# Queries and keys of seven unpadded heads to an output, their rows sent to padded tiles; scores in six banks

## The chip, the cores and the metric

The kernel runs on one core of a Trainium2 chip. The metric is device time in microseconds (us), the median of three runs. Engines are named as in the profile: PE is TensorE (matrix products), PEld its weight loads, DVE is VectorE, ACT is ScalarE, POOL is GpSimd and SP is SyncE, which here issues most DMA transfers. SBUF has 128 partitions; the accumulators (PSUM) have eight banks of 128 x 512 f32 values.

## The reference

The input x is 4 sequences (B) of 512 tokens (T) with 288 features (C), all in f32, with one condition vector for each sequence. Four layers follow one another:

- layer 0: a conditioned block whose feed-forward part is a mixture of four experts, two of them used by each token;
- layer 1: a conditioned block with a dense feed-forward part;
- layer 2: a rotation of each token within a subspace of 64 dimensions, by a matrix exponential of the condition;
- layer 3: a conditioned block like layer 1, with weighted layer norms.

The change touches the attention, which is the same in layers 0, 1 and 3 (H = 16 heads of D = 18 features):

```
h   = layernorm(x) * (1 + scale) + shift            # scale, shift, gate from the condition
q, k, v = h @ Wq + bq, h @ Wk + bk, h @ Wv + bv      # each (4, 512, 288), cut into 16 heads of 18
a   = softmax(q @ k^T / sqrt(18))                    # (4, 16, 512, 512)
x   = x + gate * ((a @ v) @ Wp + bp)
```

## The kernel before

**Tiling.** Tokens come in tiles of P = 128 (NT = 4 to a sequence). Features stand transposed, in three chunks: two of 128 rows (MC = 2) and a remainder of RR = 32, which is kept four times, once on each strip of 32 partitions (`rows_of`, line 237). A product over all features is therefore a product with 32 rows and two with 128.

**Rounds.** The attention works in 16 rounds r, one for each pair of a sequence b and a group g of four heads (NG = 4, GH = 4). A head is padded from 18 to DP = 32 rows, so four heads fill 128 partitions and head i of the group stands on strip i. Round r computes, one round ahead, the queries and keys of round r + 1 (`queries_and_keys`, line 969): two outputs of 128 rows (s = 0 queries, s = 1 keys), each one product with the remainder and four with 128 rows over half of the tokens. ACT adds the bias and copies the output to a tile that has already the padded layout (line 996).

**Scores.** The maximum of a row is subtracted before the exponential, and by a trick: the keys have a row of ones at the padding row D, and `shift` (line 1053) turns the maxima over and subtracts them from the padding row of the queries. So the scores are computed twice: `row_max` (line 1002) has queries against keys, with DVE taking the maximum, and `weight` (line 1015) has keys against the shifted queries, with ACT taking the exponential. Each is one product of 32 rows with 512 columns in a bank of its own, of the tag "sc", which has four banks. The tag "de" has three, for all other products, and one bank ("av") holds the sums.

**Order.** A round has 8 gaps k. Every product that goes through `mm` is chained to the one before it, so PE's order is that of the code. Each gap begins with a quad: `quad` (line 1028) takes the two row maxima of gap k and two weights that lag by 9 gaps, in turn. A half quad n covers token tile n // 2 and heads n % 2 * 2 and n % 2 * 2 + 1:

```
for k in range(2):
    for what, r, n in halves:
        t, i = n // 2, n % 2 * 2 + k
...
quad([(row_max, r, k)] + lagging(8 * r + k - 9))
```

After the quad come the steps of the gap (layer norms, divisions and so on for DVE and POOL), then in gaps 1 and 5 the `sums` (line 1038: weights times values, four heads on four strips of columns), and then other products by a string such as "QQQ" or "XX", each letter one step of a job: Q is queries and keys, A the transposed activations of the next sequence, X the values or a projection. `shift` of a round stands at its end, behind gap 7. `others` (line 1174) writes these plans. Values (line 937) and projections (line 1139) take two token tiles at a time in two "de" banks, with their two remainder products beside each other on two strips.

**After the sums.** `collect` (line 1083) sends the rows of each head from the padded layout to an unpadded one, by transfers on POOL's queue; `invert` and `divide` normalise; `project` multiplies with Wp and adds to x through DVE and POOL.

**Weights.** `attention_weights` (line 253) loads them by SP. The host pads the columns of Wq and Wk to 32 a head, so their tile has 2 x 1024 columns. The weights of layers 1 and 3 are loaded during the feed-forward stage ahead of them, those of layer 0 at the start.

Of the kernel before, what the change touches and what calls it, by code (L numbers as in the profile page):

```python
# [23 lines left out]
HC = P // D  # L24
OR = 64
# [21 lines left out]
def kernel(ctx: ExitStack, tc: tile.TileContext, a: dict, out: bass.AP):  # L47
# [19 lines left out]
    banks = {"sc": 4, "de": 3}  # L67

    def bank(tag, name):
        return psum.tile([P, 512], F32, tag=tag, name=name, bufs=banks[tag])  # L70
# [104 lines left out]

    cT = cst.tile([CP, KC, B], F32, tag="cT", name="cT")
# [75 lines left out]

    def attention_weights(l):

        w = {}
        w["qk"] = wt.tile([P, MC, 2 * NG * P], F32, tag="wqk", name=f"wqk{l}")
        w["qkr"] = wt.tile([2 * RR, NG * P], F32, tag="wqkr", name=f"wqkr{l}")
# [3 lines left out]
        w["bqk"] = wt.tile([P, 2 * NG], F32, tag="bqk", name=f"bqk{l}")  # L261
# [7 lines left out]
        def qk():  # L269
            load(w["bqk"], a[f"bqk{l}"])  # L270
            full_chunks(w["qk"], a[f"wqk{l}"])
# [6 lines left out]
        def qk_rest():  # L278
            for s in range(2):
                remainder(w["qkr"], a[f"wqk{l}"][:, :, s * NG * P : (s + 1) * NG * P], [s])  # L280

        def projection(g):
# [4 lines left out]
        return w, [  # L287
            qk,
            qk_rest,
            lambda: full_chunks(w["v"], a[f"wv{l}"]),  # L290
            lambda: remainder(w["v"][:, MC], a[f"wv{l}"], range(P // RR)),
            whole_rows,
        ] + [lambda g=g: projection(g) for g in range(NG)]
# [622 lines left out]
    def attention(l, w, mod, eps, feed, ticks, hT=None, then=None, also=()):  # L916
# [11 lines left out]
        with ExitStack() as es:  # L928
            pool = es.enter_context(tc.tile_pool(name=name, bufs=2))
            hTs, xns, vs, qks, raws, outs, gbs = {}, {}, {}, {}, {}, {}, {}  # L930
            dens, ps = {}, {}
# [5 lines left out]
            def values(b, t0):  # L937

                yield
                if t0 == 0:  # L940
                    vs[b] = pool.tile([P, NT, H, D + 1], F32, tag="v", name=f"{name}v{b}")
                    nc.gpsimd.memset(vs[b][:, :, :, D : D + 1], 1.0)
                ps = [bank("de", f"{name}psv{b}_{t0 + n}") for n in range(2)]

                def product(n, c):
                    q = slice((t0 + n) * P, (t0 + n + 1) * P)
                    mm(
                        ps[n][:, 0:C],
                        lhsT=rows_of(hTs[b], c, n, q),
                        rhs=rows_of(w["v"], c, n, slice(0, C)),  # L950
                        start=(c == MC),
                        stop=(c == MC - 1),
                    )

                for n in range(2):
                    product(n, MC)
                for n in range(2):
                    for c in range(MC):
                        yield
                        product(n, c)  # L960
                    o = vs[b][:, t0 + n, :, 0:D]
                    i = ps[n][:, 0:C].rearrange("p (h d) -> p h d", d=D)
                    if "bv" in w:
                        bv = w["bv"].rearrange("p (h d) -> p h d", d=D)
                        nc.vector.tensor_add(o, i, bv)
                    else:
                        nc.vector.tensor_copy(o, i)

            def queries_and_keys(r):

                yield
                b, g = groups[r]
                ps = [bank("de", f"{name}psqk{r}_{s}") for s in range(2)]
                for s in range(2):
                    rows = slice(s * RR, (s + 1) * RR)
                    mm(
                        ps[s],
                        lhsT=w["qkr"][rows, g * P : (g + 1) * P],
                        rhs=hTs[b][rows, MC, :],
                        start=True,  # L980
                        stop=False,
                    )
                for s in range(2):
                    j = s * NG + g
                    for q in (slice(0, T // 2), slice(T // 2, T)):
                        for c in range(MC):
                            yield
                            mm(
                                ps[s][:, q],
                                lhsT=w["qk"][:, c, j * P : (j + 1) * P],  # L990
                                rhs=hTs[b][:, c, q],
                                start=False,
                                stop=(c == MC - 1 and q.stop == T),
                            )
                    t = pool.tile([P, T], F32, tag=f"qk{s}", name=f"{name}qk{r}_{s}", bufs=tags["qk0"])
                    nc.scalar.activation(t, ps[s], AF.Identity, bias=w["bqk"][:, j : j + 1])  # L996
                    qks[r, s] = t
# [4 lines left out]
            def row_max(r, t, i):  # L1002
# [5 lines left out]
                    lhsT=qks[r, 0][heads_rows(i), t * P : (t + 1) * P],  # L1008
                    rhs=qks[r, 1][heads_rows(i), :],
# [5 lines left out]
            def weight(r, t, i):  # L1015
# [3 lines left out]
                    lhsT=qks[r, 1][heads_rows(i), t * P : (t + 1) * P],  # L1019
                    rhs=qks[r, 0][heads_rows(i), :],  # L1020
# [32 lines left out]
            def shift(r):  # L1053
# [12 lines left out]
                q = qks[r, 0]  # L1066
# [72 lines left out]
            def project(b, t0):  # L1139

                yield
                o = outs[b, "o"]
                ps = [bank("de", f"{name}pp{b}_{t0}_{n}") for n in range(2)]

                def product(n, c):
                    t = t0 + n * NT // 2
                    if c < MC:
                        rows, q = slice(0, HC * D), c * T + t * P  # L1150
                    else:
                        rows, q = slice(n * OR, n * OR + (H - MC * HC) * D), MC * T + t0 * P
                    mm(
                        ps[n][:, 0:C],
                        lhsT=o[rows, q : q + P],
                        rhs=w["p"][rows, c, :],
                        start=(c == MC),
                        stop=(c == MC - 1),
                    )

                for n in range(2):
                    product(n, MC)
                for n in range(2):
                    for c in range(MC):
                        yield
                        product(n, c)
                    t = t0 + n * NT // 2
                    add_gated(ps[n][:, 0:C], gbs[b], b * NT + t, f"{name}r{b}_{t}")
# [5 lines left out]
            def others(r):  # L1174
# [7 lines left out]
                pieces = {0: "QQ", 2: "QQQ", 3: "QQQ", 4: "XQX", 6: "XX", 7: "X"}  # L1182
# [9 lines left out]
                if r + 1 < n:  # L1192
                    jobs["Q"] = queries_and_keys(r + 1)
# [7 lines left out]
                if g == 1 and b + 1 < B:  # L1201
                    jobs["A"] = activations(b + 1)
                    jobs["X"] = values(b + 1, 0)
                    pieces = {0: "QQA", 2: "QQQ", 3: "QQQ", 4: "QAA", 6: "XXX", 7: "XX"}
                if g == 2 and b + 1 < B:
                    jobs["X"] = values(b + 1, 2)


                if g == 2 and 0 < b <= B:
                    steps[1].append(lambda: divide(b - 1, 0))  # L1210
                    steps[2].append(lambda: divide(b - 1, 1))
                    steps[3].append(lambda: divide(b - 1, 2))
                if 0 <= r - 2 < n:
                    steps[4].append(lambda: invert(r - 2))
                if g == 3 and b > 0:
                    jobs["X"] = project(b - 1, 0)
                if g == 0 and b > 1:
                    jobs["X"] = project(b - 2, 1)
                if "X" not in jobs:
                    pieces = {0: "QQ", 2: "QQ", 3: "QQ", 4: "QQ", 6: "Q"}  # L1220
                if "Q" not in jobs:
                    pieces = {0: "X", 2: "X", 3: "X", 4: "X", 6: "X"}
# [18 lines left out]
            def places_of_first():  # L1241

                for f in range(NF):
                    q = f * feed.width % T
                    if q == 0:
                        n = f * feed.width // T
                        tag = f"qk{n % 2}" if n < 4 else "p"
                        t = pool.tile([P, T], F32, tag=tag, name=f"{name}f{f}", bufs=tags[tag])
                    yield t[:, q : q + feed.width]

            tags = {"qk0": 3, "qk1": 3, "p": 10}

            loads = feed.loads(l)
            first = [queries_and_keys(0)]
# [17 lines left out]
            jobs["X"], jobs["Y"] = values(0, 0), values(0, 2)  # L1272
            started(jobs)
            for t, pieces in enumerate(("QQQQ", "QQQQQ", "XXXXX", "YYYYY")):
# [6 lines left out]
            shift(0)  # L1281
            for r in range(1, n):
                jobs, pieces, steps = others(r)
# [3 lines left out]
                for k in range(gaps):  # L1287
                    quad([(row_max, r, k)] + lagging(8 * r + k - 9))
                    for step in steps[k]:
                        step()  # L1290
                    if k == 1 and r > 1:
                        sums(r - 2, 2)
                        sums(r - 2, 3)
                    if k == 5:
# [3 lines left out]
                    if k == gaps - 1:  # L1298
# [3 lines left out]
                        shift(r)  # L1302
# [4 lines left out]

            jobs, _, steps = others(n)
            jobs["A"] = feed.activations()
            started(jobs)  # L1310
            for k in range(NT + 1):
                quad(lagging(8 * n + 2 * k - 9) + lagging(8 * n + 2 * k - 8))
# [24 lines left out]
            for t in range(NT // 2):  # L1337
                drain(project(B - 1, t))
# [195 lines left out]
    class Dense(Feed):  # L1534
# [4 lines left out]
        def __init__(self, l, mod, eps, func, store):  # L1539
# [5 lines left out]
            self.hTs, self.gbs = {}, {}  # L1545
# [18 lines left out]
        def event(self, b, f):  # L1564

            if b + 1 < B and f == 2:
# [18 lines left out]
    class Experts(Feed):  # L1585
# [400 lines left out]
        def beside(self, r, jobs, pieces, spaced):  # L1986
# [18 lines left out]
            if r == 15:  # L2005
                pieces = {0: "X", 2: "XX", 3: "XX"}
# [402 lines left out]
    w, loads = attention_weights(0)  # L2409
    for load in loads:  # L2410
# [8 lines left out]
    w, loads = attention_weights(1)  # L2419
    mod, work = modulation(1)  # L2420
    aside.append(work)
    hT, also = feed.finish(1, mod, 1e-6, loads)
# [4 lines left out]
    w, loads = attention_weights(3)  # L2427
# [115 lines left out]
```

## Time and profile before

| what | value |
|---|---|
| runs | 1925.31, 1916.68, 1925.64 us; median 1925.31 |
| the profiled execution | 1924.44 us, of it a span of 1922.7 us on the core |
| granted PE clock | 0.988 of full speed |
| PE busy | 1871.0 us (97%) |
| DVE, ACT, POOL busy | 1068.9 us (56%), 737.4 us (38%), 528.4 us (27%) |
| layer 0's attention | about 25 to 412 us of the span |
| layer 1's attention | about 850 to 1204 us |
| layer 3's attention | about 1407 to 1757 us |

The page gives busy times by engine, and groups of instructions by line, engine and tile; the rows of the score products are called a0m, a0s (a1m, a3m and so on) after layer and kind, those of the outputs for queries and keys a0psqk, of the values a0psv, of the projections a0pp, of the sums av. All products have one line (79), that of the helper `mm`, so they are told apart by tile. In the timeline a line has its start, its length, engine, operation, and "out<-in" with partitions x columns. A matrix product in f32 leaves two records. Ends of PE's records are modelled, so intervals are read from start to start. In answers by windows a row has the stretch, its length, the busy time of PE, PEld, DVE, ACT and POOL (with the count of instructions), the granted clock, the share of the DMA engines and GB/s.

### The profile page before, as it was taken

To read this page: it belongs to the slowest core of one execution; us is meant where nothing else is said; L and a number is where in the kernel's file an instruction comes from. 1 tells how busy PE (TensorE), PEld (TensorE's weight loads), DVE (VectorE), ACT (ScalarE), POOL (GpSimd) and SP (SyncE) were. 2 spreads that over 40 slices of the span, in tenths; PEclk is the share of its full clock that TensorE was granted. 3 is DMA by queue.
4 is the path that set the end of the run, shared out by engine and by line. 5 is a ranking of instruction groups with operands and counts; after the bars stand their busy time and mean duration, and the time that the engine had idled before them with its cause. 6 is when DMAs were issued, how large, how long until landed. Compare 5 with 4: busy or idle time off the path is not lost. (4 is left out here: it accounts for less than half of the span.)

```text
span 1922.7 us, 28265 instructions
## 1 busy us (share of the span) xinstructions
PE 1871.0 (97%) x10397; PEld 997.7 (52%) x10397; DVE 1068.9 (56%) x3158; ACT 737.4 (38%) x1353; POOL 528.4 (27%) x766
## 2 busy tenths in 40 slices
PE   8989999999999999999999999999999999999998
PEld 4434443346767777774344433555654444434565
DVE  5667777825535554657767668162365666563201
ACT  1545454443222222224555455221134555455121
POOL 2131322234334357612322123111501121222101
PEclk9999999989999999999999999999999999999999
DMA  6321122325777667621211111300001111111000
GB/s 175 77 38 41 17 58 56 85 56 181 186 223 204 174 194 222 197 78 31 47 31 29 29 34 20 73 13 5 23 1 21 37 30 27 26 29 20 19 18 23
DMA packets 86989, 136.93 MB, mean 71 GB/s; under 512 B 32292, under 2 KB 67663, under 8 KB 86851
## 3 DMA queue, kind: packets, MB, share of 16 engines
q1 hardware_dynamic: 63554, 61.46, 14.1%
q0 software_dynamic: 23184, 73.66, 13.5%
q8 instruction: 82, 1.34, 0.3%
q14 instruction: 57, 0.46, 0.1%
q10 hardware_dynamic: 112, 0.01, 0.0%
HBM read 103.25 MB, written 20.08 MB: 64 GB/s over the span
## 5 line engine op out<-in xcount | busy, mean ns | idle before, releaser
L1013 DVE TENSOR_REDUCE max<-a3m 128x1 f32<-128x512 f32 x256 | 164.6, 686 | 121.7 <-PE a3s L79 114.8
L1013 DVE TENSOR_REDUCE max<-a1m 128x1 f32<-128x512 f32 x256 | 164.3, 684 | 90.8 <-PE a1s L79 84.7
L1013 DVE TENSOR_REDUCE max<-a0m 128x1 f32<-128x512 f32 x256 | 165.1, 683 | 80.9 <-PE a0s L79 71.3
L1025 ACT ACTIVATE a0p<-a0s 128x512 f32<-128x512 f32 x256 | 140.8, 596 | 155.7 <-PE a0s L79 155.4
L1025 ACT ACTIVATE a1p<-a1s 128x512 f32<-128x512 f32 x256 | 140.0, 596 | 139.3 <-PE a1s L79 139.3
L1025 ACT ACTIVATE a3p<-a3s 128x512 f32<-128x512 f32 x256 | 139.7, 596 | 136.0 <-PE a3s L79 136.0
L79 PE MATMUL e0h<-e0hT,e0w 128*128 128x256 f32 (+1 forms) x918 | 171.0, 397 | 2.8 <-DMA e0w<-w1c,wrow 0.9
L79 PE MATMUL a0m<-a0qk,a0qk 32*128 32x512 f32 x512 | 164.0, 650 | 9.6 <-DVE max L1013 8.2
L79 PE MATMUL e0o<-e0w,e0hm 128*128 128x288 f32 x648 | 169.9, 412 | 2.0 <-DVE ef L881 2.0
L79 PE MATMUL a0s<-a0qk,a0qk 32*128 32x512 f32 x512 | 166.7, 657 | 0.0
L79 PE MATMUL a1m<-a1qk,a1qk 32*128 32x512 f32 x512 | 153.3, 640 | 3.1 <-DVE max L1013 1.7
L79 PE MATMUL a1s<-a1qk,a1qk 32*128 32x512 f32 x512 | 154.9, 640 | 0.0
L79 PE MATMUL a3m<-a3qk,a3qk 32*128 32x512 f32 x512 | 151.2, 640 | 2.3 <-ACT a3qk L996 0.8
L79 PE MATMUL a3s<-a3qk,a3qk 32*128 32x512 f32 x512 | 153.0, 643 | 0.0
L79 PEld LDWEIGHTS e0h<-e0hT,e0w 128*128 128x128 f32 (+1 forms) x918 | 130.2, 191 | 37.3 <-issue 15.7
L79 PEld LDWEIGHTS e0o<-e0w,e0hm 128*128 128x128 f32 x648 | 121.1, 192 | 34.0 <-DVE ef L881 2.4
L1451 ACT ACTIVATE e0hm<-e0h,e0w 128x256 f32<-128x256 f32 x144 | 60.6, 471 | 124.3 <-PE e0h L79 117.0
L660 POOL TENSOR_TENSOR nrm<-n,phalf 64x1 f32<-64x1 f32 (+34 forms) x35 | 19.3, 552 | 285.9 <-DVE n L655 285.8
L2011 POOL DMA_INDIRECT e0w<-w1c,wrow x57 | 55.8, 980 | 120.9 <-PE e0h L79 57.1
L79 PEld LDWEIGHTS a0m<-a0qk,a0qk 32*128 32x128 f32 x512 | 48.9, 185 | 72.5 <-DVE max L1013 40.0
L79 PE MATMUL f1h<-f1hT,w 128*128 128x512 f32 (+1 forms) x216 | 81.3, 616 | 0.4 <-ACT f1hT L535 0.4
L79 PE MATMUL f3h<-f3hT,w 128*128 128x512 f32 (+1 forms) x216 | 79.4, 613 | 0.4 <-ACT f3hT L535 0.4
(534 smaller groups left out, 3191.4 us busy)
## 6 DMA issues: line engine op xcount, KB each, us to landing
eo<-e0r SPq DMA_DIRECT2D x50, 144.0 KB
ada<-in_ada SPq DMA_DIRECT2D x18, 324.0 KB
wr<-in_wrot SPq DMA_DIRECT2D x16, 288.0 KB
xm<-e0m SPq DMA_DIRECT2D x6, 768.0 KB
g<-gates SPq DMA_DIRECT2D x24, 144.0 KB
w<-in_w SPq DMA_DIRECT2D x6, 432.0 KB
x<-in_x SPq DMA_DIRECT2D x16, 144.0 KB
w1c<-in_w SPq DMA_DIRECT2D x8, 288.0 KB
```

The source lines that it names most:

```text
L79: ins = nc.tensor.matmul(*args, **kwargs).ins
L660: in_turn("POOL", nc.gpsimd.tensor_tensor(nrm, n2, phalf[0:n], ALU.pow))
L1013: take("DVE", nc.vector.tensor_reduce(m[:, t, i, D : D + 1], ps, AX.X, ALU.max))
L1025: take("ACT", nc.scalar.activation(p, ps, AF.Exp, scale=D**-0.5))
L1451: nc.scalar.activation(self.hms[i][f], ps[r], func, bias=b1(f)),
L2011: gather = nc.gpsimd.indirect_dma_start(dst, None, table, bass.IndirectOffsetOnAxis(row, 0))
```

## The change

The columns of queries and keys lose their padding. The 32 heads of a sequence (16 of queries and 16 of keys, group by group, queries of a group ahead of its keys) are cut into NP = 5 outputs of up to HC = 7 heads (126 rows). An output is copied with its bias to a tile of 126 rows, and each head's 18 rows go by a transfer of their own to a persistent padded tile `pads`, which has places for three rounds (NR = 3) of queries and of keys. The keys' padding row of ones is set once; the queries' tile is cleared again by POOL before each round, since `shift` writes into its padding rows. A head whose place is still in use waits in a list until `sent` issues it one round ahead of its use.

The scores take their banks from a ring of six (four "sc" and two of the three "de") while the rounds run. Values, projections and outputs for queries and keys take one "de" bank at a time, and values and projections one token tile at a time, so remainders no longer stand in pairs, but for the last sequence's projections. A round has one output for queries and keys in gaps 3 and 4, and the last round of a sequence two. Two tiles of values and the first two outputs stand ahead of round 0.

`shift` moves from the end of a round to behind the first quad of the next; the weights lag by 10 gaps instead of 9; the sums move from gaps 1 and 5 to 2 and 6. The plans of `others` are rewritten, with P for projections.

The loaded weights are still padded on the host. They are loaded into `pads` and copied without padding to their tile: by POOL for layer 0, by ACT in the preceding stage for layers 1 and 3, which clear `pads` again by DVE. The remainder's weights and the biases are loaded head by head.

```diff
+NP = -(-2 * H // HC)
+NR = 3
...
+    ring, turns, wide = ["sc"] * 4 + ["de"] * 2, [0], [False]
+    def single(tag, name):
+        return psum.tile([P, 512], F32, tag=tag, name=name, bufs=banks[tag])
     def bank(tag, name):
-        return psum.tile([P, 512], F32, tag=tag, name=name, bufs=banks[tag])
+        if wide[0]:
+            turns[0] += 1
+            tag = ring[turns[0] % len(ring)]
+        return single(tag, name)
...
+    pads = cst.tile([P, 2 * NR, T], F32, tag="pads", name="pads")
+    def cleared(engine, k):
+        if k < NR:
+            engine.memset(pads[:, k, :], 0.0)
+        else:
+            engine.tensor_copy(pads[:, k, :], unit.to_broadcast([P, T]))
...
+    def heads_of(n):
+        got = []
+        for q in range(n * HC, min((n + 1) * HC, 2 * H)):
+            g, s, i = q // (2 * GH), q // GH % 2, q % GH
+            if got and got[-1][0:2] == [g, s]:
+                got[-1][3] += 1
+            else:
+                got.append([g, s, i, 1, q - n * HC])
+        return got
+    def rest_of(n):
+        r = n % (P // RR)
+        return slice(r * RR, (r + 1) * RR), n // (P // RR) * HC * D
...
+        staged = [pads[:, 1:NR, :], pads[:, NR + 1 :, :]]
+        def compact(copy, c, s):
+            own = w["qk"][:, c, :].rearrange("p (g s i d) -> p g s i d", g=NG, s=2, d=D)
+            padded = staged[c][:, s, :].rearrange("p (g i e) -> p g i e", g=NG, e=DP)
+            copy(own[:, :, s], padded[:, :, :, 0:D])
...
+            def place(what):
+                return misc(what) if now[1] else single("de", what)
...
+            def send(r, s, i, row, queue):
+                to = pads[i * DP : i * DP + D, s * NR + r % NR, :]
+                queue.dma_start(to, row)
+            def sent(r):
+                for one in [one for one in waiting if one[0] == r]:
+                    waiting.remove(one)
+                    send(*one, nc.gpsimd)
-            def queries_and_keys(r):
+            def queries_and_keys(*some):
+                for b, n in some:
+                    yield
+                    ps = place(f"{name}psqk{b}_{n}")
+                    m = min(HC, 2 * H - n * HC) * D
+                    rows, first = rest_of(n)
...
+                    t = pool.tile([HC * D, T], F32, tag="qk", name=f"{name}qk{b}_{n}", bufs=3)
+                    nc.scalar.activation(
+                        t[0:m], ps[0:m], AF.Identity, bias=w["bqk"][0:m, n : n + 1]
+                    )
+                    for g, s, i, k, at in heads_of(n):
+                        for j in range(k):
+                            row = t[(at + j) * D : (at + j + 1) * D, :]
+                            one = (b * NG + g, s, i + j, row)
+                            if one[0] < NR or one[0] <= now[0] + 1:
+                                queue = nc.scalar if s and one[0] == 0 else nc.gpsimd
+                                send(*one, queue)
+                            else:
+                                waiting.append(one)
...
-                    lhsT=qks[r, 0][heads_rows(i), t * P : (t + 1) * P],
-                    rhs=qks[r, 1][heads_rows(i), :],
+                    lhsT=pads[heads_rows(i), r % NR, t * P : (t + 1) * P],
+                    rhs=pads[heads_rows(i), NR + r % NR, :],
...
-                pieces = {0: "QQ", 2: "QQQ", 3: "QQQ", 4: "XQX", 6: "XX", 7: "X"}
+                pieces = {1: "PPP", 3: "QQ", 4: "QQQ", 5: "PP", 7: "P"}
...
+                if g < NG - 1 and b < B:
+                    jobs["Q"] = queries_and_keys((b, g + 2))
+                elif b + 1 < B:
+                    jobs["Q"] = queries_and_keys((b + 1, 0), (b + 1, 1))
...
+                if g == 3 and b + 1 < B:
+                    pieces = {0: "Q", 1: "QQQQ", 3: "QQ", 4: "QQQ", 5: "PP", 7: "P"}
+                    if b == 0:
+                        pieces = {0: "Q", 1: "QQQQ", 3: "QQ", 4: "Q", 5: "Q", 7: "Q"}
...
+                if NR <= r + 1 < n:
+                    steps[1].append(lambda: cleared(nc.gpsimd, (r + 1) % NR))
+                if r + 1 < n:
+                    steps[1].append(lambda: sent(r + 1))
...
-            first = [queries_and_keys(0)]
+            first = [queries_and_keys((0, 0), (0, 1)), values(0, 0, 1)]
...
-                    quad([(row_max, r, k)] + lagging(8 * r + k - 9))
+                    quad([(row_max, r, k)] + lagging(8 * r + k - 10))
+                    if k == 0:
+                        shift(r - 1)
...
-                    if k == 1 and r > 1:
+                    if k == 2 and r > 1:
                         sums(r - 2, 2)
                         sums(r - 2, 3)
-                    if k == 5:
+                    if k == 6:
                         sums(r - 1, 0)
                         sums(r - 1, 1)
...
-                        shift(r)
```

## The prediction

> **What bounds the kernel now.** I read the page's busy line first, then three stretches (the attention layers l = 0, 1, 3), then the timeline of TensorE (PE) inside layer 3. Each f32 product shows as two PE records, one after the other.
>
> ```profile
> PE 1871.0 (97%) x10397; PEld 997.7 (52%) x10397; DVE 1068.9 (56%) x3158; ACT 737.4 (38%) x1353; POOL 528.4 (27%) x766
> ...
> 36.00:412.00 376.00, 363.02 (x2188) 154.95 (x2187) 270.60 (x729) 178.55 (x320) 90.96 (x139) 0.97 0.27 58
> 850.00:1204.00 354.00, 347.43 (x2104) 146.79 (x2104) 255.05 (x602) 177.44 (x314) 91.99 (x140) 1.00 0.15 32
> 1407.00:1757.00 350.00, 345.68 (x2105) 146.61 (x2106) 217.29 (x413) 177.16 (x315) 63.77 (x105) 1.00 0.13 25
> ```
>
> PE is busy 97 to 99% of each attention layer, VectorE (DVE) 62 to 72%, ScalarE (ACT) about half. So what PE issues there sets the time, and each gap of a round is a sum of PE blocks:
>
> ```profile
> 1530.27 1.03 PE L79 MATMUL a3psqk<-a3hT,wqkr 32*128 32x512 f32 x4
> 1531.23 0.70 PE L79 MATMUL a3psqk<-a3hT,wqk 128*128 128x256 f32 x2
> 1531.86 0.69 PE L79 MATMUL a3m<-a3qk,a3qk 32*128 32x512 f32 x1
> 1531.86 0.69 PE L79 MATMUL a3s<-a3qk,a3qk 32*128 32x512 f32 x1
> 1531.87 0.69 PE L79 MATMUL a3m<-a3qk,a3qk 32*128 32x512 f32 x1
> 1531.88 0.69 PE L79 MATMUL a3s<-a3qk,a3qk 32*128 32x512 f32 x1
> 1532.39 0.59 PE L79 MATMUL a3m<-a3qk,a3qk 32*128 32x512 f32 x1
> 1532.39 0.59 PE L79 MATMUL a3s<-a3qk,a3qk 32*128 32x512 f32 x1
> 1532.40 0.59 PE L79 MATMUL a3m<-a3qk,a3qk 32*128 32x512 f32 x1
> 1532.41 0.59 PE L79 MATMUL a3s<-a3qk,a3qk 32*128 32x512 f32 x1
> 1532.93 1.91 PE L79 MATMUL av<-a3p,a3v 128*19 128x512 f32 x16
> 1534.77 0.69 PE L79 MATMUL a3m<-a3qk,a3qk 32*128 32x512 f32 x1
> ```
>
> A quad (two row-max products a3m, two weights a3s) takes 1.07 us to the next block: all four first records start together, all four second ones 0.53 us later. They can, because the four stand on four different strips of 32 partitions. In `quad` the head is i = n % 2 * 2 + k. The row max takes n = gap; the weight lags by 9 gaps, so its n has the other parity: strips 0, 2, 1, 3, or 2, 0, 3, 1.
>
> What a strip used twice costs is seen where the experts issue nine 32-row products in a row on strips 0 1 2 3 0 1 2 3 0:
>
> ```profile
> 579.86 1.15 PE L79 MATMUL e0h<-e0hT,e0w 32*128 32x256 f32 x16
> 580.83 0.59 PE L79 MATMUL av<-e0hT,e0w 32*128 32x256 f32 x2
> 581.35 0.48 PE L79 MATMUL e0h<-e0hT,e0w 128*128 128x256 f32 x1
> ```
>
> Eight products two deep take 0.97 us, and the ninth, third on its strip, 0.52 more, about 0.09 of it the change of shape after it. A level of 256 columns is thus some 0.43 us, one of 512 columns 0.86.
>
> **The change part by part.** The sum is made against the profiled execution: 1924.4 us, a span of 1922.7 and 1.7 around it, 0.9 under the median of the three runs, which I neglect.
>
> 1. *The lag of 10 gaps.* `quad` is not in the diff, but the weights now lag by 10 gaps, an even number. Row max and weight have n of one parity and so the same i: the quad's order becomes strip i, i, i+1, i+1. Only two of four strips work, each two products deep. There are 6 such quads in round 1 and 8 in each of rounds 2 to 15: 118 a layer, 354 in all. (Round 0 and the tail pair n and n+1 and are as before.) The second level costs 0.86 us by the experts' rows, 0.77 by the av rows above (1.84 us for two deep on four column strips, against 1.07 for one). I take 0.86, the same strips of rows: 354 x 0.86 = **+304** (273 at the low end). This needs the third product, whose strip is free, to start beside the first although the second stands before it. The trace shows something near it: the first records of products two to four start before the second record of product one, and where a second pair came late (1547.97, against 1547.71) it too began before the first pair's second records at 1548.24.
>
> The skill's page "TensorE: Matmul & The Clock Gate" (Part 3, What overlaps and what doesn't) says that matrix products start in strict program order and only weight loads are pulled ahead. The rows above look freer than that, if the two records of a product stand together in the program. By the rule the quad would be a staircase of three levels, 2.79 us, and the sum some 300 us higher.
>
> 2. *Waits of the quads.* Summed over the timeline, the 129 score blocks of each layer take 164.2, 151.5 and 149.7 us to the next block; 387 at 1.07 would be 414, so 51 us are waits for banks (a max or an exp of the quad before). Longer quads and six banks remove most: **-35** (0 to -51).
>
> 3. *Queries and keys.* Before, a round's two outputs are 10 products in blocks of 1.59 (two remainders beside each other and a full product, 1530.27 to 1531.86), 1.49, 1.49 and 0.54 us (the last beside the values, 1541.44 to 1541.98): 5.1 us, in 15 rounds 77 a layer. After, an output is one remainder and four full products, 1.59 + 1.49 = 3.08 us, and 18 of the 20 lie in the rounds: 55. Two outputs stand ahead of the rounds in both, now with remainders one after the other (+1). So -20.5 a layer, **-61**. The remainder stands on strip n % 4; for 18 or so of the 54 outputs the quad before leaves that strip free: x 0.86, **-15** (0 to -18).
>
> 4. *One bank at a time.* Two value tiles were 0.59 + 0.58 + 1.17 + 0.59 = 2.93 us with their remainders side by side (1540.86 to 1549.62); alone each is 0.59 + 1.17: +0.59 a pair, 8 pairs a layer, +14. A projection pair was 0.69 + 0.58 + 1.17 + 0.59 = 3.03 (1562.14 to 1571.00) and becomes 2 x 1.86: +0.69, six pairs a layer, +12. Together **+26**.
>
> 5. *Gaps with nothing between two quads* (8 or so a layer: no projection in rounds 1, 4, 5, 13, 14). The next quad has the other two strips and can run beside: 24 x up to 0.86, **-15** (0 to -20).
>
> 6. *Rows sent to padded tiles.* 128 transfers a layer of 18 rows of 2 KB, most on POOL's queue, and a clear of 128x512 for each of 13 rounds. Rows for these:
>
> ```profile
> a3oo<-a3raw POOLq DMA_DIRECT2D x56, 36.0 KB, 1.8
> ...
> 2.11 0.53 POOL L171 MEMSET max<- 128x512 f32 x1
> ...
> 9.65 1.65 SPq L193 DMA_DIRECT2D wqkr<-in_wqk  x2
> 11.35 5.75 SPq L193 DMA_DIRECT2D wv<-in_wv  x8
> ```
>
> An issue on POOL takes 0.51 us (median of layer 3's 72), so 72 us of POOL a layer, where POOL is busy 18 to 26%: hidden. The tightest deadline: an output ends in gap 4, its copy takes 0.69 (the a3qk row), seven issues 3.6, the landing 1.8: 6.1 us, against three gaps of 2.6 now and some 3.4 after. If POOL is held by the collect transfers or gated adds queued ahead of the sends, PE's next row max waits. In round 3 of batch 0 the second output ends only in gap 7. I allow **+10** (0 to 30) for late heads. The start of each layer waits for the first heads (0.69 + 4 x 0.51 + 1.8 = 4.5 us, under two value tiles of 3.5): +1 each. In layer 0 SP issues 19 more small loads (11 for the remainder rows instead of 2, 11 biases instead of 1) ahead of wv, at 0.4 to 0.8 us some 10 us; wv's issue, over at 17.1 now, ends near 27, and the value products, first needed at 34.8 now, are due near 25. With POOL's four copies of wqk (0.8 us each at most, by its 0.80 us adds of 128x288): +7. Together **+10** (0 to 20).
>
> 7. *Banks.* A product that holds a "de" bank over two gaps stands in the same rotation of three as a third of the scores; the score that comes round to it waits for the copy (0.69). One half us a round: **+10** (0 to 25). The shift moves by a gap with the lag, with the one gap between it and the first weight as before: 0. The clears and copies of weights for layers 1 and 3 lie in the expert and dense stages on ACT, DVE and POOL, which are idle half the time there: 0; if that cover is gone, 8 copies of under 0.7.
>
> Sum: 304 - 35 - 61 - 15 + 26 - 15 + 10 + 10 + 10 = +234 us: **2158**. With every term at its low end it is 2073, at its high end 2268.
>
> **The rivals.**
> - *A, the staircase.* The third product waits behind the second, so a quad has three levels: 1.07 + 2 x 0.86 = 2.79 us. Another 354 x 0.86 = 304: about 2462. If the third waits only until the second's weights may be loaded, half of it: 2310. For it: nothing in this trace has order i, i, j. Against it: the interleaved records.
> - *B, late heads.* POOL's queue stands still behind its waits (the collect transfers waited 129 us for the av copy in layer 3, POOL being idle). Two us a round in 45 rounds: +90 in place of part 6's 10, about 2240.
> - *C, faster.* The same strip costs nothing: the quad stays at 1.07, because what makes the four run together is not their strips. Then the 304, and the strip gains of parts 3 and 5, fall away: 1924 - 35 - 61 + 26 + 30 = 1884, or 1838 if the waits go wholly and nothing new comes. It decides where a quad stays under about 1.18 us (1.07 + 40 / 354). Against it: the ninth expert product began only when its strip was free.
> - *D, half hidden.* The second level runs beside the following block, so it costs 0.4 us a quad: 2158 - 354 x 0.46 = about 1995. Against it: every block with another shape starts 0.11 us later than one of the same shape (1.07 against the 0.97 from 1529.30 to 1530.27), as if PE emptied first.
>
> **How the numbers follow.** Forecast 58% (its own range 2073 to 2268, the ends of its terms), A 18% (half of it at 2310), B 9%, C 9%, D 6%. The range 2060 to 2380 leaves out A's far half, C and D, and holds the rest but for a little of B's and the forecast's edges. Slower by over 0.5% (about what a measurement of this kernel can tell): 0.90; faster 0.08; the same 0.02.
>
> **What would show it.** Right: in the timeline of layers 0, 1 and 3 only two of a quad's four products start together, the next block is some 1.9 us after the quad's first, and each layer's stretch grows by 60 to 95 us; the full psqk records fall from 256 to 160 a layer; DVE's share there falls. Rival A: one product, then two, then one, 2.8 us. B: PE waits for transfers into the padded tiles. C: quads at 1.07. Wrong most easily if the strips of one quad differ after all.

## The result, and the profile after

The changed kernel takes 2176.31 us (median of 4 runs, 2158.1 to 2182.13) against 1920.99 us before (4 runs, 1914.83 to 1925.64). The ratio is 1.131, with a 95% interval of 1.127 to 1.135. The forecast was 2158 us, in a range of 2060 to 2380.

The profiled execution took 2182.13 us, with a span of 2180.4. The page's busy line, and the three attention layers by windows (columns as before: stretch, its length, PE, PEld, DVE, ACT and POOL busy with counts, granted clock, DMA share, GB/s):

```profile
PE 2118.3 (97%) x10037; PEld 1077.0 (49%) x10037; DVE 1099.8 (50%) x3171; ACT 713.8 (33%) x1325; POOL 737.7 (34%) x1187
...
37.00:485.00 448.00, 440.80 (x2108) 180.32 (x2107) 285.23 (x749) 169.68 (x308) 156.67 (x269) 0.95 0.27 64
...
943.00:1387.00 444.00, 439.89 (x1971) 175.53 (x1969) 263.93 (x602) 167.96 (x300) 156.73 (x269) 0.92 0.15 35
...
1597.00:2015.00 418.00, 410.88 (x1970) 167.01 (x1970) 225.71 (x412) 167.75 (x301) 128.14 (x234) 0.98 0.14 31
```

PE has fewer products (10037 records instead of 10397) and is as busy as before, over a longer time. DVE's share in the layers fell to between 54 and 64%. In the timeline of layer 3 a quad now reads:

```profile
1651.05 1.13 PE L89 MATMUL a3m<-pads 32*128 32x512 f32 x4
1652.01 1.03 PE L89 MATMUL a3s<-pads 32*128 32x512 f32 x4
1652.97 1.91 PE L89 MATMUL av<-a3p,a3v 128*19 128x512 f32 x16
```

The two row maxima (four records) run together, and only 0.96 us later the two weights; the next block starts 1.92 us after the quad's first, where it was 1.07. The order of the program is max, weight, max, weight: the third product has started ahead of the second, whose strip was taken. The timeline shows this even across jobs:

```profile
1641.61 0.70 PE L89 MATMUL a3m<-pads 32*128 32x512 f32 x2
1641.64 1.07 PE L89 MATMUL a3psqk<-a3hT,wqkr 32*72 32x512 f32 x2
1642.14 0.60 PE L89 MATMUL a3m<-pads 32*128 32x512 f32 x2
1642.57 1.03 PE L89 MATMUL a3s<-pads 32*128 32x512 f32 x4
1643.53 0.65 PE L89 MATMUL a3psqk<-a3hT,wqk 128*72 128x256 f32 x2
```

A remainder product (a3psqk, on strip 0) starts beside the maxima of a quad (strips 2 and 3), though the quad's weights stand before it in the program. The 1.92 us is no single case: it is the median of the 254 quads of the three layers that run at full clock with another block on either side.

Where the time went, from the two traces (a layer counts from its first score product to the end of its last score block; "half clock" is the time that the trace grants PE half of full speed):

| stretch, us | before | after |
|---|---|---|
| start, up to the first score product | 25.4 | 37.1 |
| layer 0's attention | 386.5 | 447.8 |
| experts | 439.0 | 458.6 |
| layer 1's attention | 352.9 | 443.5 |
| dense stage of layer 1, and the rotation | 203.6 | 210.1 |
| layer 3's attention | 348.9 | 417.5 |
| half clock in the whole span | 47 | 178 |

Within the layers, and up to the next block, scores went from 465.5 to 757.0 us, outputs for queries and keys from 238.8 to 153.8, values from 69.9 to 68.7, projections from 61.3 to 77.1, shifts from 42.8 to 29.4. Of 258 us, some 220 lie in the three layers and 37 outside. Of the 37, 11 are work that moved: two tiles of values now stand ahead of the first score product of each layer, as here in layer 1. From its first output for queries and keys to its first score product a layer now takes 9.6 to 9.9 us, where it was 5.6 to 6.2.

```profile
939.83 3.76 PE L89 MATMUL a1psv<-wv,a1hT 32*128 32x288 f32 x12
943.52 1.14 PE L89 MATMUL a1m<-pads 32*128 32x512 f32 x8
```

What I had not reckoned with is the clock. One stretch of it by windows, in layer 1:

```profile
1310.00:1331.70 21.70, 21.70 (x101) 7.57 (x100) 13.62 (x31) 9.21 (x17) 7.00 (x15) 1.00 0.17 36
1331.70:1369.00 37.30, 37.30 (x92) 11.72 (x92) 12.73 (x33) 6.61 (x12) 5.39 (x8) 0.50 0.06 9
```

The granted clock is 0.50 for 37 us in which the trace shows no gap on PE.

### The profile page after: what moved, and what is told of

It reads as the page before. It is cut to its first block, busy times and chain, and to the rows that moved or that the text cites. A ratio compares the mean times of both kernels' runs of the same rounds, so it can differ in the third digit from the quotient of the medians.

```text
span 2180.4 us, 28654 instructions
## 1 busy us (share of the span) xinstructions
PE 2118.3 (97%) x10037; PEld 1077.0 (49%) x10037; DVE 1099.8 (50%) x3171; ACT 713.8 (33%) x1325; POOL 737.7 (34%) x1187
## 5 line engine op out<-in xcount | busy, mean ns | idle before, releaser
L89 PE MATMUL a1m<-pads 32*128 32x512 f32 x512 | 156.3, 678 | 3.1 <-issue 2.4
L89 PE MATMUL a0m<-pads 32*128 32x512 f32 x512 | 152.7, 671 | 2.8 <-DMA pads<-a0qk 2.4
L89 PE MATMUL a3m<-pads 32*128 32x512 f32 x512 | 144.5, 649 | 5.1 <-DMA pads<-a3qk 5.1
L89 PE MATMUL a1s<-pads 32*128 32x512 f32 x512 | 143.8, 629 | 0.1
L89 PE MATMUL a0s<-pads 32*128 32x512 f32 x512 | 140.1, 610 | 1.4 <-ACT a0p L1125 1.4
L89 PE MATMUL a3s<-pads 32*128 32x512 f32 x512 | 135.5, 601 | 0.4 <-ACT a3p L1125 0.4
L1053 POOL DMA_DIRECT2D pads<-a3qk x124 | 62.3, 508 | 100.8 <-ACT a3qk L1086 79.2
L1053 POOL DMA_DIRECT2D pads<-a0qk x124 | 62.8, 512 | 78.3 <-ACT a0qk L1086 61.4
L193 POOL MEMSET pads<- 128x512 f32 x42 | 22.0, 525 | 193.5 <-PE a1s L89 75.5
L89 PEld LDWEIGHTS a1s<-pads 32*128 32x128 f32 x512 | 55.7, 196 | 63.5 <-issue 53.5
```

The lines of the kernel that those rows point to most:

```text
L89: ins = nc.tensor.matmul(*args, **kwargs).ins
L193: engine.memset(pads[:, k, :], 0.0)
L1053: queue.dma_start(to, row)
```

## The experiments

The theory: a quad's products share strips because of the lag of 10 gaps, and this sharing is nearly the whole loss. The rivals: the transfers and loads of the change, or the clock, made it slow. Each time below is a median, each ratio is against the kernel before on the same chip.

### The other strips

```diff
             else:
+                i = (1 - n % 2) * 2 + k
                 ps[r, t, i] = weight(r, t, i)
```

> The changed kernel with one line more: a weight's half of the heads is swapped (heads 2 and 3 for even n, 0 and 1 for odd n), so that a quad's weights stand on the two strips that its row maxima leave free; the lag stays at 10 gaps. Theory (the strips are the cost): a quad's block falls from 1.92 us to 1.07, 354 x 0.85 = 301 us go, and with what the other parts gained before (61 for fewer outputs, 26 given back for single tiles, some 30 for start and late heads) the time is about 1885 us, 1850 to 1915. Rival (late heads of the padded tiles, or the lower granted clock, hold the time up): it stays above 2050 us, with the stretches at half clock as they were (178 us of the span).

Measured: 1937.7 us, ratio 1.011 (1.007 to 1.015). The line takes back 239 us. A quad is again four together, as this stretch of its timeline shows:

```profile
1599.84 0.69 PE L89 MATMUL a3m<-pads 32*128 32x512 f32 x1
1599.84 0.69 PE L89 MATMUL a3s<-pads 32*128 32x512 f32 x1
1599.85 0.69 PE L89 MATMUL a3m<-pads 32*128 32x512 f32 x1
1599.86 0.69 PE L89 MATMUL a3s<-pads 32*128 32x512 f32 x1
...
1600.91 0.75 PE L89 MATMUL a3pp<-wp,a3oo 126*128 126x288 f32 x2
```

But 1885 was expected, 1915 at most. Half clock is still 102 us. The layers (382.8, 341.9, 344.0) are 20 us shorter in all than before, while start (37.3), experts (452.9) and dense stage (207.9) are 30 longer, 11 of it the values that moved. Within the layers the outputs for queries and keys are 85 us shorter, and the scores' blocks 57 longer (522 against 465.5). Part of both is named by the waits of PE (engine, tile and line; what it waited for; us in total, times, longest):

```profile
PE psr L896 <- DMA wr<-in_wrot: 11.4, 2, 6.5
PE a3m L89 <- DMA pads<-a3qk: 10.1, 2, 6.6
PE psada L473 <- DMA ada<-in_ada: 8.0, 2, 5.5
PE a1m L89 <- issue: 5.7, 1, 5.7
PE a0m L89 <- DMA pads<-a0qk: 4.0, 1, 4.0
```

The pads rows are heads that come late, rival B of the prediction; the row named "issue" is one too, by its place (round 4 of layer 1, two sends issued at 953.5, the score at 958.4). The psr and psada rows are weights of the rotation and the modulation; in the kernel before PE waited 3.0 us for the rotation's. The edits "Heads sent earlier" and "Weights without padding" below go after these.

### The kernel before, with the same strips

The same line in the kernel before: with its lag of 9 it puts the weights on the strips of the maxima.

> The kernel before with the same line, which there does the opposite: with a lag of 9 gaps the swapped halves put the weights on the strips of the row maxima. Nothing else of the change is in it. Theory: 354 x 0.85 = 301 us more, less up to 50 us of waits of the quads: about 2195 us, 2150 to 2260; and the time at half clock grows from 47 us of the span towards the changed kernel's 178, since the same strips are idle. Rival (the outputs, transfers and banks of the change made it slow): within 1% of 1921 us.

Measured: 2173.21 us, ratio 1.132 (1.127 to 1.137), the changed kernel's own loss. Its timeline has the same quads (0.96 to the weights, 1.92 to the next block):

```profile
1701.51 1.13 PE L79 MATMUL a3m<-a3qk,a3qk 32*128 32x512 f32 x4
1702.47 1.03 PE L79 MATMUL a3s<-a3qk,a3qk 32*128 32x512 f32 x4
1703.43 0.70 PE L79 MATMUL a3psqk<-a3hT,wqk 128*128 128x256 f32 x2
```

The score blocks sum to 732.6 us, 267 more than before; terms 1 and 2 of the prediction made that 304 - 35 = 269. What missed is the clock: 45 us at half clock, where it was 47. So two strips alone do not lower it here. And since the strips alone cost as much as the whole change, the gains and losses of the rest of it come to about nothing.

### Another order on the same strips

```diff
-for k in range(2):
-    for what, r, n in halves:
+for what, r, n in halves:
+    for k in range(2):
```

> The changed kernel with the four products of a quad in another order: both row maxima (strips i, i+1), then both weights (strips i, i+1). Theory (each strip works through its own products, whatever stands between them in the program): no change, within 1% of 2176 us, quads at 1.92 us. Rival (products are started in the order of the program, and part of the cost is a third product that waits behind the second): up to 5% faster.

Measured: 2178.95 us, ratio 1.131 (1.125 to 1.138). No change, and the median quad is 1.92 us again: what counts is how many products stand on a strip, not their order.

### Four banks for the scores

```diff
-ring = ["sc"] * 4 + ["de"] * 2
+ring = ["sc"] * 4
```

This is on top of the other strips.

> The first of these kernels with the ring of banks cut back to the four of tag sc; everything else as there. Theory: with four strips at work a quad fills all four banks and the next waits for a maximum and an exponential, as in the kernel before (51 us of waits in its three layers): 20 to 50 us slower than the first. Rival (the waits are hidden by other products in every gap): within 0.5% of it.

Measured: 2025.43 us, ratio 1.055 (1.050 to 1.060), 88 us over the kernel with six banks. The direction is right and the size twice what I allowed: score blocks sum to 597.9 us against 522.1, and half clock is 132 us against 102. I had taken the waits of the kernel before as the measure; these plans have fewer other products in a gap to cover a maximum and an exponential. That cause is argued, not shown.

### Heads sent earlier

On top of the other strips:

```diff
-                    if b == 0:
-                        pieces = {0: "Q", 1: "QQQQ", 3: "QQ", 4: "Q", 5: "Q", 7: "Q"}
...
-                    pieces = {1: "Q", 3: "Q", 4: "Q", 5: "QQ"}
+                    pieces = {1: "Q", 3: "QQ", 4: "QQ"}
```

> The kernel with the other strips (1937.7 us), and two lines of the plans changed: the output that ends in gap 7 of round 3 (sequence 0) and the one that ends in gap 5 of the last round but one now end in gap 4, so that their heads are sent two or three gaps earlier. Theory (late heads: PE waits 4.0, 5.7, 3.5 and 6.6 us for padded tiles at the start of the round after these, and each of these waits is followed by 7 to 14 us at half clock): 20 us of waits and some 20 us of slow clock go, so about 1900 us, 1890 to 1920, and the time at half clock falls from 102 us to under 70. Rival (the waits move to the gaps that now lack other products, as maxima and exponentials bind there): within 0.5% of 1937.7.

Measured: 1916.51 us, ratio 0.997 (0.994 to 0.999): 21 us go, half of what was expected. Half clock falls from 102 to 81 us, where under 70 was expected. The layers are 372.9, 336.7 and 336.1 us, 23 shorter together. The waits that it removes looked like this, in layer 3 of the kernel with the other strips:

```profile
1720.52 1.50 POOL L1053 DMA_DIRECT2D pads<-a3qk  x3 [2.86 <-issue]
...
1727.61 1.19 PE L89 MATMUL a3m<-pads 32*128 32x512 f32 x1 [6.63 <-DMA pads<-a3qk]
```

Three heads, issued at 1720.5, are waited for by PE until 1727.6: 5.6 us after the end of the last issue, where the median landing is 1.8. In layers 1 and 3 eight transfers of the next stage's weights had been put on SP's queue just before the like waits (950.4 and 1494.8 to 1503); that these delayed the landings was not tried apart. In the case shown, SP had issued no weights since 1706.9, and the gates' rows that it issued at 1719.6 came as late (POOL got them at 1727.3); what delayed these stays open.

One more wait went: that of 5.5 us for the modulation's weights in layer 0 is 1.0 here.

### Weights without padding

On top of the other strips: the host lays the weights and biases of queries and keys out by groups of four heads without padding. The kernel loads them straight to their tiles; staging, copies and the small loads go.

```diff
-        first = [lambda: qk(0), lambda: qk(1), qk_rest, biases]
-        first += [compacted(nc.gpsimd.tensor_copy, c) for c in range(MC)]
...
+        def qk():
+            full_chunks(w["qk"], a[f"wqk{l}"])
+        def biases():
+            load(w["bqk"][0 : HC * D], a[f"bqk{l}"])
+        def qk_rest():
+            own = a[f"wqk{l}"][CP - RR : CP, KC - 1]
+            for n in range(NP):
+                rows, first = rest_of(n)
+                m = min(HC, 2 * H - n * HC) * D
+                load(w["qkr"][rows, first : first + m], own[:, n * HC * D : n * HC * D + m])
...
+            clear(nc.gpsimd, 0, 1, 2)()
+            late = [clear(nc.vector, NR, NR + 1, NR + 2)]
```

> The kernel with the other strips, and the weights and biases of queries and keys laid out without padding in DRAM: they load with 10 transfers a layer (4, 5 and 1) instead of 26, nothing is staged in the padded tiles and nothing copied by POOL or ACT. The attention is as it was. Theory (that kernel's layers are 20 us shorter than in the kernel before, and its start 11.6, its expert stage 13.9 and its dense stage 4.3 us longer, because SP's queue holds the rotation's and modulation's weights behind the small loads and POOL's copies hold the first layer norm): 20 to 30 us go, about 1912 us, first score product at 25 to 27 us instead of 37. Rival (the transfers of heads, not the loads, cost it): within 0.5% of 1937.7.

Measured: 1911.13 us, ratio 0.995 (0.993 to 0.997): 27 us go. The first score product comes at 27.5 us, the expert stage is back at 438.4 (439.0 before), and the waits for the rotation's weights are gone. The dense stage stays at 208.1, 4.5 over the kernel before; 3.8 of it is the values that moved (9.63 us from the first output of layer 3 to its first score product, 5.84 before). The wait for the modulation's weights in layer 0 stays too, at 5.8 us. What held the start up is seen in the timeline of the changed kernel, POOL first and then SP:

```profile
9.22 0.61 POOL L195 COPY pads<-unit 128x512 f32<-128x512 f32 x1 [5.00 <-DVE unit L188]
...
16.57 0.82 POOL L322 COPY wqk<-pads 128x288 f32<-128x288 f32 x2
17.30 1.01 POOL L193 MEMSET pads<- 128x512 f32 x2
18.23 0.80 POOL L322 COPY wqk<-pads 128x288 f32<-128x288 f32 x2
18.97 1.17 POOL L195 COPY pads<-unit 128x512 f32<-128x512 f32 x2
20.10 1.04 POOL L580 TENSOR_TENSOR ln_0rstd<-ln_0ve,mhalf 128x4 f32<-128x4 f32 x1
```

```profile
8.33 7.41 SPq L305 DMA_DIRECT2D wqkr<-in_wqk  x11
15.79 7.56 SPq L305 DMA_DIRECT2D bqk<-in_bqk  x11
23.39 4.14 SPq L215 DMA_DIRECT2D wv<-in_wv  x8
```

POOL first stands still for 5.0 us behind DVE for the row of ones, and then copies weights and clears tiles ahead of the first layer norm's power, which runs at 20.1 us instead of 12.3. PE waits until 21.9 us for the layer norm. The 22 small loads take 15 us of SP's queue.

### Both edits

> Both edits together on the kernel with the other strips. Theory (the costs lie in different stages and add): about 1880 us, 1865 to 1895, 2% under the kernel before, which is what seven heads to an output were priced at. Rival (late heads come from transfers that share the engines with the next stage's weights, whatever the plan): above 1905 us.

Measured: 1887.38 us, ratio 0.982 (0.979 to 0.985). The two gains add (21 + 27 expected, 50 measured). This beats both kernels, by 34 us the one before; whether it is 2% under that, as expected, the interval leaves open. Of the waits for heads one of 3.3 us is left:

```profile
PE a3m L89 <- DMA pads<-a3qk: 3.3, 1, 3.3
```

The layers are 374.2, 337.5 and 334.7 us, 42 shorter than in the kernel before. The expert stage is 445.5 in the profiled execution (1895 us, the longest of the four), 7 longer than with the unpadded weights alone, with a wait of 4.0 us for the rotation's weights.

### Both edits, on the same strips

The last kernel without the line of the first experiment.

> The last kernel (1887.4 us) without the line that moved the weights to the other strips: the changed kernel with its earlier outputs and its unpadded weights. Theory (the strips, the late heads and the loads are separate costs, and the long stretches at half clock come from the waits for late heads): 1887 + 250 = 2137 us, 2120 to 2155, with less than 110 us at half clock. Rival (the low clock goes with two strips in plans that leave gaps without other products): still over 150 us at half clock, and the time above 2155.

Measured: 2106.79 us, ratio 1.098 (1.091 to 1.105), with 73 us at half clock. The rival falls, but the time is below the range that was expected: the strips cost 219 us here, fewer than the 239 and 251 of the other two pairs. Against the changed kernel 70 us and 106 us of half clock are gone; halving the clock for 106 us costs at most 53. Every execution shows this fall: the mean clock is 0.959 to 0.972 in the changed kernel and 0.976 to 0.988 here. So two strips do not bring the slow clock by themselves: with both edits it is 73 us on two strips and 74 on four, without them 178 and 102. That two strips lengthen it beside late heads and loads is not shown beyond these two traces.

## Why the prediction was right, and where not

*The bound, and step 1.* Right. PE sets the time of the layers; a quad went from 1.07 to 1.92 us, the price taken from the experts' rows was 1.93. The second experiment has this step alone: 251 us by the medians, against 269 for steps 1 and 2. Rival A (the staircase) falls with the 1.92 and with the unchanged time of the other order. Rival D (half hidden) falls too, as it had a quad cost 0.4 us more, and 0.85 was measured. Rival C needed a quad under 1.18 us.

The rule of the Trainium skill's page "TensorE: Matmul & The Clock Gate" (Part 3, What overlaps and what doesn't) was set against rows of the trace in the prediction. The rows decide: on strips of their own, products of f32 start ahead of products that stand before them, as the remainder at 1641.64 does.

*Step 3.* Right in size: -85 us in the blocks where -61 - 15 was reckoned.

*Step 4.* Right: +15 us in the layers (values -1, projections +16) and 11 for the two value tiles of each layer that had moved ahead of the first score product (3.7 us each time), against +26.

*Step 5.* Wrong in the main. In the rounds 21 pairs of quads at full clock stand together with nothing between them. The median pair takes 3.81 us, against 2 x 1.92 = 3.84, and all 21 together save some 4 us where 15 were reckoned. In three places the second quad does run beside the first (2.96 us for the pair). Mostly only part of it does, as here in layer 1:

```profile
1324.16 1.15 PE L89 MATMUL a1m<-pads 32*128 32x512 f32 x6
...
1325.12 1.04 PE L89 MATMUL a1s<-pads 32*128 32x512 f32 x6
...
1326.06 0.29 PEld L89 LDWEIGHTS a1m<-pads 32*128 32x128 f32 x2 [0.73 <-DVE max L1113]
1326.06 1.12 PE L89 MATMUL a1m<-pads 32*128 32x512 f32 x2
```

Six of the eight records of maxima start at once. The last two, of the second quad, start only at 1326.06, when DVE is done with a maximum of the first. The step had left out the banks: a quad takes four, so a ring of six holds one quad and a half.

*Step 6.* Right for the heads: 10 us were allowed, and in the changed kernel PE waits 9.9 us for them (5.1, 2.4 and 2.4). With the other strips, where the quads are shorter, it waits 20, and two plans that send heads earlier take 21 off. The places were named rightly too (the output that ends in gap 7). The start was allowed 7 + 1 us, and the first output for queries and keys does come 8.1 us later (27.2 against 19.15), but by another way: through POOL to the first layer norm, not through SP's queue to the values. The right size is luck there. What the step had wrong are the loads for layers 1 and 3, costed at 0. The expert stage is 19.6 us longer, 4 of it work that moved, and its waits for the rotation's weights grew from 3.0 to 9.5 us; with the small loads they went. The step had counted engines' time and not SP's queue. All loads together are worth 27 us with the other strips.

*Step 7.* The +10 us for waits in the shared ring was not measured by itself. The ring as a whole is worth 88 us on four strips; on two, no run has it apart. The shift, costed at 0, became 13 us shorter.

*Not in the sum.* Half clock rose from 47 to 178 us. At half speed that is up to 65 us lost, which no term of the sum has. The total came within 1% of the median all the same (2158 against 2176), so the rest of the sum came out lower than reckoned by up to 45 us or so. Shifts (13) and outputs (9) account for half of that, while loads and step 5 went the other way; the rest cannot be told apart from the clock. That the total is so near is luck; that the strips make up nearly all of it is not.

What stays open: what sets off the slow clock in each place. In the changed kernel 12 of 18 stretches begin in a wait of PE of 0.8 us or more, or within 2 us of one, but they hold only half of the time (89 of 178 us). The others begin with PE at work, the longest (37 us) where a layer ends in quads with little between them.

## What to carry to other kernels

Where several small products share PE by strips of partitions, a lag or a reordering by one step can put them on the same strip; the price here is one more product's length for each level (0.85 us a quad), and it shows in the timeline, where products that started together now start one level later. Check which strip each product stands on whenever an index that chooses it moves, and swap one index rather than the lag. When a wait on a transfer is added to a full PE, look for the clock behind it, and count small loads by the queue that issues them and who stands behind them there.

## What the runs showed of the hardware

- Waits of PE of 2 to 7 us are often followed by half clock, for 3 to 20 us (in the changed kernel 5.1 us at 1959.8, then 20.5 us from 1963.2). In the kernel before a wait of 3.6 us was followed by 3.4, one of 2.7 by 6.8.
- The clock can halve while the trace shows no gap on PE: 37 us from 1331.7 in the changed kernel, where quads on two strips and the shift were the only products in the 7 us ahead of it.
- A product of 32 rows on a free strip starts ahead of earlier ones that wait for theirs, across jobs too (the remainder at 1641.64, ahead of weights at 1642.57).
- Transfers of a head (18 rows of 2 KB) landed 1.8 to 2.6 us after their issue in the median of a layer, and now and then more than 5 (5.6 us after the last issue of 1720.5, with the other strips).
